# Two-layer graph network on one core: the sums over keys move from TensorE to DRAM gathers and VectorE

## The chip, the cores and the metric

The kernel runs on one core of a Trainium2 chip (trn2). The metric is the device time of one execution in microseconds (us), as the median of the runs. The engines are named as the profile has them: PE is TensorE (PEld its weight loads), DVE VectorE, ACT ScalarE, POOL GpSimd, SP SyncE, which here only issues DMAs (SPq is its queue).

## The reference

64 batch elements of 256 tokens with 512 features go through two layers. The first is multi-head attention under a mask, the second a graph attention with a rank-one score; both end in a residual and a layer norm. Everything is fp32.

```python
q, k, v = x @ Wq + bq, x @ Wk + bk, x @ Wv + bv        # 8 heads of 64
scores = einsum('bqhd,bkhd->bhqk', q, k) / 8 + (1 - adj) * -1e9
out = einsum('bhqk,bkhd->bqhd', softmax(scores), v) @ Wo + bo
x = layernorm(x + out)
h = x @ W
e = leaky_relu(s1[:, :, None] + s2[:, None, :], 0.2) * adj   # s1 = h @ a1, s2 = h @ a2
x = layernorm(x + elu(softmax(e) @ h + beta * h))
```

## The kernel before, in words

**Work and tiling.** Batch elements go in 32 pairs (m); an element is b = 2m + s. For a pair, `project` (L414) makes q, k and v, each 512 x 512 features on 512 tokens, with seven products of quarters in place of eight (sums and differences of quarters on both sides, as in Winograd's form of Strassen's scheme). The same helper is used per element for o (Wo), for spread (attention of the second layer times x) and for u (times W). The sums on the right side are made on GpSimd by `token_sums` (L393); the sums of weights once, at the start.

**Left sides.** Those of q and k are streamed: `streamed` (L358) makes four sums of quarters on DVE, stores them in DRAM, and from the second pair on each product fetches its left side (256 KB) into one of six slots named piece, in program names `wq_sums` and `wk_sums` (L381 from the weight itself, L386 from the stored sums). Wv, Wo and W stay in SBUF, with three sums each from `weight_sums` (L344, on POOL).

**First attention, by keys.** `scores` (L734) puts keys on partitions and queries in columns, so that exp of it, pT (8 heads of 128 x 2 x 256), can multiply v without a transpose. DVE adds the mask (L750), ACT takes the exponential (L752), POOL adds the two halves of keys into both (L754). The sum over the 128 keys on partitions is a product with ones: `denominators` (L758) runs eight matmuls into ps_den (L766), 32 columns wide, four at a time. Then DVE takes the reciprocal (L778), ACT adds up both for a check of range (L774, kept in range_sb), and the reciprocals go through DRAM to all partitions: rows<-inv (L786), inv_all<-rows (L790, two DMAs). ps_pv (L720) is pT times v; DVE multiplies it by inv_all (L816) into oT, POOL makes oS from it, and o follows. The last element takes another way without DRAM: ps_inv (L802).

**Second layer.** DVE makes the two scores of a token (L917), which go through DRAM to rows (L941, L943); e is formed on DVE, POOL and ACT (L946 to L966), transposed in blocks through DRAM (square L983, att_b L986, DVE L990), and used by spread. The last element has transposes on TensorE in place of both trips (L933, L976).

**What sets the order.** No scheduler of the compiler works here: all operations go into `Plan` (L54) with an engine, a cost in ns and what they read and write; `place` lists them. TensorE's order is fixed by turns: each operation has the round m + LATER[what] and its place in ROUND (L23); only its last 60 are free. The other engines take what can start, by due time counted back from TensorE's. A DMA is planned as landing 4.2 us after its issue. Every engine then executes its own list strictly in order, SP too: an issue that waits holds those behind it. Slots (L242) bound how far the lists run ahead; PSUM has 8 banks (`ps`), of which ps_sc takes two for each pair of heads, `project` three or four.

One line of code shows the product with ones:

```python
nc.tensor.matmul(acc[32 * c:32 * c + 32, :], ones[:, 16 - 16 * i:48 - 16 * i],
                 both[c][:, i, :], start=i == 0, stop=i == 1)
```

Of the kernel before, what the change touches and what calls it, by code (L numbers as in the profile page):

```python
# [12 lines left out]
ALU = mybir.AluOpType  # L13
# [3 lines left out]
P = 128  # L17
# [5 lines left out]
ROUND = ("sums1", "mix1", "scores0", "spread1", "v", "u1", "attention0", "sums0", "mix0", "scores1", "o1", "x",  # L23
         "logits1", "q", "spread0", "o0", "attention1", "u0", "k", "logits0")
# [3 lines left out]
         "u0": 1, "u1": 2}  # L28
SAFE = 1e15
# [198 lines left out]
def gnn_two_layers(ctx: ExitStack, tc: tile.TileContext, x, adj, Wq, bq, Wk, bk, Wv, bv, Wo, bo, W, a, beta, out):  # L228
# [13 lines left out]
    slots = {"xin": 2, "x": 4, "two": 6, "xP": 1, "piece": 6, "full": 4, "half": 18, "xS": 2, "st": 76, "ps": 8, "rows": 4, "svT": 4, "line": 4, "square": 4}  # L242
# [69 lines left out]
    wv_sb = weight(Wv, "wv_sb")  # L312
# [13 lines left out]
    range_sb = once([2, B], "range_sb")  # L326
    maskT_sb = once([NT, N], "maskT_sb")
# [30 lines left out]
    def streamed(w, w_dram, name):  # L358
# [4 lines left out]
        for n, to, p, m, op, reads in ((3, s3, w11, w21, ALU.subtract, [w]), (1, s1, w21, w22, ALU.add, [w]),  # L363
                                       (2, s2, s1, w11, ALU.subtract, [w, S[1]]),
                                       (4, s4, w12, s2, ALU.subtract, [w, S[2]])):
            plan.op("DVE", 700, lambda to=to, p=p, m=m, op=op: nc.vector.tensor_tensor(to(), p(), m(), op), reads,
                    [S[n]])
# [46 lines left out]
    def project(left, right, by_feature, claims, copy, add, inner=2, width=P, raw=False):  # L414
# [35 lines left out]
        if raw:  # L450
            add((0, 0), pe(2, second, True))
            copy((1, 0), pe(4, fourth, True))
        copy((1, 1), pe(5, cross, True))
        if not raw:
            add((0, 0), pe(2, second, True))
        copy((0, 1), pe(6, chain, False))
        add((0, 1), pe(3, cross, False))
        if not raw:
            copy((1, 0), pe(4, fourth, True) if second[1] is None else pe(4, fourth, False, [second]))
# [69 lines left out]
    def second_layer_constants():  # L529
        plan.op("POOL", 500, lambda: nc.gpsimd.memset(diag_sb[A], 0.0), [], [diag_sb])  # L530
# [53 lines left out]

    def pair(m, at, general=False):

        def turn(what):

            plan.turn = ((m or 0) + LATER[what], ROUND.index(what))
# [47 lines left out]
        def qk(left, bias, dst):  # L637
            project(left, right, True, [dst], *gather(
                lambda q: (lambda: dst[:, 2 * q[0]:2 * q[0] + 2, q[1] * N:(q[1] + 1) * N], (dst, q)), bias, True),
                width=N, raw=m == 0)  # L640

        if m == 0:
            wq_sb, wk_sb = sb("two", [C, D], "wq_sb"), sb("two", [C, D], "wk_sb")
            load(wq_sb, Wq)
            load(wk_sb, Wk)
            lq, left["q"] = streamed(wq_sb, Wq, "wq_sums")
# [7 lines left out]
            left["v"] = weight_sums(wv_sb, "sv_sb", "POOL")  # L654
            plan.turn = (0, ROUND.index("x"))
            left["o"] = residual_bias()
        else:
# [5 lines left out]
        project(left["v"], right, False, [V], *gather(  # L663
            lambda q: (lambda: V[:, 2 * q[1]:2 * q[1] + 2, half(q[0])], (V, q)), wide=True), width=N)
# [3 lines left out]
    def batch(m, s, qT, kT, V, dram, general):  # L668

        b = None if m is None else 2 * m + s  # L670
        last = b == B - 1 and not general
        X = sb("x", [NT, D], f"x_{b}")

        def turn(what):
            plan.turn = ((m or 0) + LATER[f"{what}{s}"], ROUND.index(f"{what}{s}"))
# [51 lines left out]
        def attention_by_keys():  # L727
# [6 lines left out]
            def scores(c):  # L734
# [4 lines left out]
                def pe():  # L739
                    for k in range(NT):  # L740
# [6 lines left out]
                        claims=pT[2 * c:2 * c + 2] + [both[c]])  # L747
                for i in range(2):
# [5 lines left out]
                    plan.op("POOL", 725, lambda h=h, i=i: nc.gpsimd.tensor_tensor(  # L754
                        both[c][:, i, :], pT[h][:, 0, :], pT[h][:, 1, :], ALU.add),
                        [pT[h]], [(both[c], i)])

            def denominators():  # L758
                turn("sums")

                acc = ps([N], "ps_den")

                def pe():
                    for i in range(2):
                        for c in range(C):
                            nc.tensor.matmul(acc[32 * c:32 * c + 32, :], ones[:, 16 - 16 * i:48 - 16 * i],  # L766
# [355 lines left out]
```

## Time and profile before

| | |
|---|---|
| median of 3 runs | 2732.69 us (2732.62 to 2733.25) |
| profiled execution, its own time | 2734.59 us |
| its span, first to last instruction | 2732.8 us |
| TensorE's granted clock, mean | 0.995 |
| busy: PE, DVE, POOL, ACT | 2698.5, 1960.9, 1728.6, 1549.5 us |
| DMA | 581,596 packets, 301.44 MB, q1 busy 41.7% of 16 engines |
| matmuls of ps_den (L766) | 1,024 records, 68.5 us busy |
| reciprocal of ps_den (L778) | 64 of 1,757 ns |

Busy time of matmuls overlaps from one to the next, and a record's end is modelled, so distances on TensorE are taken from start to start. A group's line gives its count, busy us and mean ns, then the engine's idle time just before it and who ended that. A matmul of fp32 with more than one pass shows as two records.

### The profile page before, as it was taken

How to read it: one execution, taken by the hardware profiler on the slowest of the kernel's cores; microseconds unless marked ns; L12 is line 12 of the kernel's file. 1: busy time of each engine (PE TensorE's matmuls, PEld its weight loads, DVE VectorE, ACT ScalarE, POOL GpSimd, SP SyncE). 2: the span in 40 equal slices, each digit the busy share in tenths (PEclk: the TensorE clock that was granted, in tenths of full speed). 3: DMA queues.
4: the chain of work that ended last, by engine and by line, in shares of the span. 5: the costliest groups of instructions: out<-in, count | busy, mean ns of one | idle time of the engine just before them, and what ended most of it. 6: DMA issues, size and time to landing. Idle time of an engine off the chain costs nothing. (4 is left out here: it accounts for less than half of the span.)

```text
span 2732.8 us, 47289 instructions
## 1 busy us (share of the span) xinstructions
PE 2698.5 (99%) x15897; PEld 2268.1 (83%) x15897; DVE 1960.9 (72%) x3676; ACT 1549.5 (57%) x3712; POOL 1728.6 (63%) x2261
## 2 busy tenths in 40 slices
PE   9999999999999999999999999999999999999996
PEld 7888888888888888888888888888888888888874
DVE  6777777777777777777777776777777777767674
ACT  3456556556556565565565565655655655656554
POOL 4756666665676666666656766666666566665663
PEclk9999999999999999999999999999999999999998
DMA  8434434344443444343443434443444434343211
GB/s 234 104 101 128 119 97 114 97 121 124 100 120 96 109 128 118 94 113 99 124 124 98 120 90 115 128 113 99 111 101 120 128 96 118 89 120 113 80 55 54
DMA packets 581596, 301.44 MB, mean 110 GB/s; under 512 B 407020, under 2 KB 512356, under 8 KB 581348
## 3 DMA queue, kind: packets, MB, share of 16 engines
q1 hardware_dynamic: 581220, 298.34, 41.7%
q8 instruction: 130, 2.13, 0.3%
q14 instruction: 118, 0.97, 0.1%
q0 software_dynamic: 128, 0.01, 0.0%
HBM read 245.50 MB, written 52.75 MB: 109 GB/s over the span
## 5 line engine op out<-in xcount | busy, mean ns | idle before, releaser
L754 POOL TENSOR_TENSOR both<-pT 128x256 f32<-128x256 f32 x512 | 361.3, 734 | 398.6 <-ACT pT L752 398.6
L750 DVE TENSOR_TENSOR pT<-ps_sc,maskT_sb 128x512 f32<-128x512 f32 x512 | 324.2, 680 | 84.7 <-PE ps_sc L743 84.7
L752 ACT ACTIVATE pT<-pT 128x512 f32<-128x512 f32 x512 | 304.0, 626 | 49.3 <-DVE pT L750 47.4
L917 DVE SCALAR_TENSOR_TENSOR junk<-x,wa_sb 128x512 f32<-128x512 f32 x256 | 207.8, 837 | 110.3 <-ACT x L581 109.2
L743 PE MATMUL ps_sc<-qT,kT 64*128 64x256 f32 x2048 | 238.4, 382 | 0.0
L720 PE MATMUL ps_pv<-pT,v 128*64 128x256 f32 x2048 | 235.1, 382 | 0.0
L743 PEld LDWEIGHTS ps_sc<-qT,kT 64*128 64x128 f32 x2048 | 192.8, 187 | 44.4 <-issue 24.6
L469 ACT COPY u<-ps_chain 128x256 f32<-128x256 f32 x126 | 47.0, 373 | 319.2 <-PE ps_chain L433 318.7
L581 ACT ACTIVATE x<-x,nmr,rs 128x512 f32<-128x512 f32 x256 | 197.6, 808 | 50.2 <-POOL nmr L577 50.0
L720 PEld LDWEIGHTS ps_pv<-pT,v 128*64 128x64 f32 x2048 | 141.3, 137 | 91.0 <-DVE kT L478 12.8
L1026 POOL TENSOR_TENSOR X_sums<-x 128x256 f32<-128x256 f32 x126 | 150.9, 1207 | 99.5 <-ACT x L581 99.5
L564 ACT ACTIVATE junk<-x,mean 128x512 f32<-128x512 f32 x256 | 182.2, 714 | 6.4 <-DVE mean L570 6.4
L564 ACT ACTIVATE junk<-x 128x512 f32<-128x512 f32 x256 | 159.4, 625 | 36.5 <-DVE x L894 33.7
L704 POOL TENSOR_TENSOR x<-x,res_sb 128x512 f32<-128x512 f32 x128 | 176.3, 1380 | 0.0
L575 POOL TENSOR_SCALAR rs<-sq 128x2 f32<-128x2 f32 x130 | 34.9, 269 | 194.3 <-ACT junk L564 189.0
L404 POOL TENSOR_TENSOR oS<-oT 128x256 f32<-128x256 f32 x126 | 92.1, 731 | 84.2 <-DVE mean L570 52.5
L816 DVE TENSOR_TENSOR oT<-oT,inv_all 128x512 f32<-128x512 f32 x126 | 134.7, 1107 | 0.0
L955 POOL TENSOR_TENSOR e<-e,adj_sb 128x512 f32<-128x512 f32 (+1 forms) x65 | 81.6, 1255 | 80.7 <-DVE e L952 76.8
L433 PE MATMUL ps_chain<-sw_sb,yS 128*128 128x256 f32 x504 | 129.3, 379 | 0.0
L433 PE MATMUL ps_chain<-so_sb,oS 128*128 128x256 f32 x504 | 129.3, 379 | 0.0
L778 DVE RECIPROCAL inv<-ps_den 128x256 f32<-128x256 f32 x64 | 112.5, 1757 | 17.1 <-PE ps_den L766 8.7
L404 POOL TENSOR_TENSOR yS<-yT 128x256 f32<-128x256 f32 x126 | 92.6, 735 | 48.5 <-DVE yT L478 32.2
(240 smaller groups left out, 7164.5 us busy)
## 6 DMA issues: line engine op xcount, KB each, us to landing
x<-in_x_dram SPq DMA_DIRECT2D x64, 512.0 KB
out_dram<-x SPq DMA_DIRECT2D x128, 256.0 KB
inv_all<-rows SPq DMA_DIRECT2D x126, 256.0 KB
xin<-in_x_dram SPq DMA_DIRECT2D x248, 128.0 KB
wq_sums<-wq_sums SPq DMA_DIRECT2D x124, 256.0 KB
wk_sums<-wk_sums SPq DMA_DIRECT2D x124, 256.0 KB
wq_sums<-in_L_gnn_Wq_dram SPq DMA_DIRECT2D x93, 256.0 KB
wk_sums<-in_L_gnn_Wk_dram SPq DMA_DIRECT2D x93, 256.0 KB
```

What stands on the lines that cost most here:

```text
L404: plan.op("POOL", 180 + 545 * width // P, lambda: nc.gpsimd.tensor_tensor(dst(), p(), m(), ALU.subtract), reads, writes)
L433: nc.tensor.matmul(dst[:, f, :], lhs, rhs, start=start and f == 0 and c == 0, stop=c == inner - 1, skip_group_check=True)
L564: plan.op("ACT", 700, lambda: nc.scalar.activation(junk[A], X[:, t, :], func, bias=mean[:, i:i + 1] if bias else 0.0, accum_out=to[:, i:i ...
L581: plan.op("ACT", 810, lambda i=i, t=t: nc.scalar.activation(X[:, t, :], X[:, t, :], AF.Identity, bias=nm[:, i:i + 1], scale=rs[:, i:i + 1] ...
L704: plan.op("POOL", 1270, lambda t=t: nc.gpsimd.tensor_tensor(X[:, t, :], X[:, t, :], res_sb[A], ALU.add), [res_sb], tokens(t))
L720: nc.tensor.matmul(acc[r * HD:(r + 1) * HD, i, :], V[:, 2 * k + s, h * HD:(h + 1) * HD], pT[h][:, k, :], start=k == 0, stop=k == NT - 1)
L743: nc.tensor.matmul(acc[j][:, k, :], kT[r:r + HD, c, key_blk(k)], own(qT, r, c), start=True, stop=True)
L750: plan.op("DVE", 690, lambda h=h, i=i: nc.vector.tensor_add(pT[h][A], acc[i][A], maskT_sb[A]), [acc[i], maskT_sb], [pT[h]])
L752: plan.op("ACT", 620, lambda h=h: nc.scalar.activation(pT[h][A], pT[h][A], AF.Exp, scale=1.0 / HD ** 0.5), [pT[h]], [pT[h]])
L754: plan.op("POOL", 725, lambda h=h, i=i: nc.gpsimd.tensor_tensor(both[c][:, i, :], pT[h][:, 0, :], pT[h][:, 1, :], ALU.add), [pT[h]], [(bot ...
L917: plan.op("DVE", 780, lambda t=t, i=i, junk=junk: nc.vector.scalar_tensor_tensor(junk[A], X[:, t, :], 1.0, wa_sb[:, i, :], op0=ALU.mult, o ...
L1026: plan.op("POOL", ns, lambda: nc.gpsimd.tensor_tensor(dst(), p(), m(), op), reads, writes)
```

## The change

- `denominators` no longer uses TensorE. The four tiles both (256 KB each) are written to DRAM as keys (128 keys x 2048 columns, a column is a head and a query). Four DMAs read them back with columns spread over partitions: few holds 32 keys x 64 columns on each partition, 32 column groups for each of four groups of keys, in runs of 64 elements (256 B). DVE adds up the 32 keys (part), which go through DRAM once more (parts, four) so that DVE can add the four groups and take the reciprocal of 64 x 32 numbers (den). Then rows and inv_all as before.
- The last pair (`near`) keeps the product with ones, straight from pT (16 matmuls for each element, no both), and both its elements have their logits and attention turned by TensorE, where before only the last element had.
- Left sides of v are streamed as those of q and k. wv_sb is a slot of two at the start only; the pieces have seven slots, not six.
- The first pair's products come in another order (`first`, before `raw`), its sums of weights too (s3 last), and diag_sb is cleared after w_sb has come.
- ROUND is another order.

```diff
-ROUND = ("sums1", "mix1", "scores0", "spread1", "v", "u1", "attention0", "sums0", "mix0", "scores1", "o1", "x",
-         "logits1", "q", "spread0", "o0", "attention1", "u0", "k", "logits0")
+ROUND = ("sums1", "mix1", "scores0", "v", "spread1", "o1", "u1", "logits1", "k", "attention0", "sums0", "mix0",
+         "scores1", "x", "q", "attention1", "spread0", "o0", "logits0", "u0")
...
-    slots = {... "piece": 6, ...}
+    slots = {... "piece": 7, ...
+             "keys": 3, "parts": 3, "few": 1, "part": 2, "four": 2, "den": 2}
...
-        if raw:
+        if first:
             add((0, 0), pe(2, second, True))
-            copy((1, 0), pe(4, fourth, True))
         copy((1, 1), pe(5, cross, True))
-        if not raw:
+        if not first:
             add((0, 0), pe(2, second, True))
         copy((0, 1), pe(6, chain, False))
-        add((0, 1), pe(3, cross, False))
-        if not raw:
-            copy((1, 0), pe(4, fourth, True) if second[1] is None else pe(4, fourth, False, [second]))
+        if not first:
+            add((0, 1), pe(3, cross, False))
+        copy((1, 0), pe(4, fourth, True) if second[1] is None else pe(4, fourth, False, [second]))
+        if first:
+            add((0, 1), pe(3, cross, False))
...
-            left["v"] = weight_sums(wv_sb, "sv_sb", "POOL")
+            lv, left["v"] = streamed(wv_sb, Wv, "wv_sums")
...
+        near = m == B // 2 - 1 and not general
...
             def denominators():
+                keys, parts = Buf(dram_pool, "keys", [P, H * N], "keys"), Buf(dram_pool, "parts", [4, H * N], "parts")
+                for c in range(C):
+                    plan.op("SP", 500, lambda c=c: nc.sync.dma_start(
+                        keys[:, 2 * c * N:2 * (c + 1) * N], both[c][A].rearrange("p i n -> p (i n)")), [both[c]],
+                        [(keys, c)])
+                few, part = sb("few", [32, 64], "few"), sb("part", [64], "part")
+                for g in range(4):
+                    plan.op("SP", 800, lambda g=g: nc.sync.dma_start(
+                        few[32 * g:32 * g + 32], keys[32 * g:32 * g + 32, :].rearrange("k (c n) -> c k n", n=64)),
+                        [keys], [(few, g)])
+                plan.op("DVE", 2200, lambda: nc.vector.tensor_reduce(
+                    part[A], few[A].rearrange("p k n -> p n k"), AX.X, ALU.add), [few], [part])
+                plan.op("SP", 500, lambda: nc.sync.dma_start(
+                    parts[A].rearrange("g (c n) -> (g c) n", n=64), part[A]), [part], [parts])
+                four, den = sb("four", [4, 32], "four"), sb("den", [2, 32], "den")
+                plan.op("SP", 500, lambda: nc.sync.dma_start(
+                    four[0:HD], parts[A].rearrange("g (c n) -> c g n", n=32)), [parts], [four])
+                plan.op("DVE", 210, lambda: nc.vector.tensor_reduce(
+                    den[0:HD, 0, :], four[0:HD].rearrange("p g n -> p n g"), AX.X, ALU.add), [four], [(den, 0)])
+                plan.op("DVE", 280, lambda: nc.vector.reciprocal(den[0:HD, 1, :], den[0:HD, 0, :]), [(den, 0)],
+                        [(den, 1)])
...
+                plan.op("SP", 500, lambda: nc.sync.dma_start(
+                    rows[A].rearrange("h (c n) -> (h c) n", n=32), den[0:HD, 1, :]), [(den, 1)], [rows])
+                to_all()
...
+            def denominators_near():
                 turn("sums")
...
-                plan.op("PE", 1000, pe, both, [acc], mode="sums", claims=[inv])
+                plan.op("PE", 1860, pe, pT, [acc], mode="sums", claims=[inv])
...
-            spread_inv = denominators()
+            spread_inv = denominators_near() if near else denominators()
...
-        if last:
+        if near:
             row = ps([N], "tr_s")
```

## The prediction

> **What bounds the kernel now.** I read the page's busy times and slices first, then the waits of TensorE, then the timeline of TensorE over a stretch in the middle, and last the groups for the lines that the diff touches. The page says TensorE is busy in every slice at its full clock, and no other engine is near that:
>
> ```profile
> span 2732.8 us, 47289 instructions
> PE 2698.5 (99%) x15897; PEld 2268.1 (83%) x15897; DVE 1960.9 (72%) x3676; ACT 1549.5 (57%) x3712; POOL 1728.6 (63%) x2261
> PE   9999999999999999999999999999999999999996
> PEclk9999999999999999999999999999999999999998
> ```
>
> "Busy" alone proves little, since matmuls overlap. The list of what TensorE waited for is better evidence: its longest entries sum to some 19 us in 2733, and every one lies in the first 90 us or the last 90 (us in total, times, longest):
>
> ```profile
> PE tr_x L608 <- DMA xin<-in_x_dram: 4.1, 2, 3.7
> PE ps_inv L802 <- DVE select L783: 2.8, 1, 2.8
> PE ps_chain L433 <- DVE attT L990: 2.5, 1, 2.5
> PE ps_fourth L433 <- POOL xS L404: 2.0, 1, 2.0
> ```
>
> So in the 31 rounds between, TensorE's own instructions set the time: a round (two batch elements) is 83.65 us, from one ps_sc at 2515.90 to that of the next round at 2599.55. An instruction taken from TensorE there shortens the run by what it occupies, as long as nothing else becomes late. What the sums over keys occupy is read from start to start (the second column, a duration, overlaps the next row):
>
> ```profile
> 1002.20 1.89 PE L433 MATMUL ps_fourth<-xS,wk_sums 128*128 128x256 f32 x8
> 1003.93 1.89 PE L433 MATMUL ps_chain<-xS,wk_sums 128*128 128x256 f32 x8
> 1005.75 1.07 PE L766 MATMUL ps_den<-both,ones 128*32 128x256 f32 x16
> 1006.75 3.67 PE L720 MATMUL ps_pv<-pT,v 128*64 128x256 f32 x32
> 1010.36 3.72 PE L743 MATMUL ps_sc<-qT,kT 64*128 64x256 f32 x32
> ```
>
> ps_den holds TensorE from 1005.75 to 1006.75: 1.00 us. The other place in the round, 1035.48 to 1036.48, gives 1.00 too.
>
> **What the Trainium skill says.** "TensorEngine Tiling (Array Packing)", Key Properties: a change of tiling mode drains TensorE. The trace agrees: a plain product takes 1.73 us from start to start, the one ahead of ps_den 1.82. That 0.09 stays, since ps_pv has a mode of its own: at 2653.70 a product of half the size goes straight into ps_pv and takes 0.96 against 0.86. "TensorE: Matmul & The Clock Gate" (Architectural detail) says that VectorE executes in strict order; so a VectorE instruction that waits for a DMA holds up all behind it. No row of before shows that for a long wait. "DMA: Bandwidth & Descriptors", Anatomy of one DMA, gives about 2 us fixed cost for a DMA; here rows<-inv is issued at 1038.43 and inv_all<-rows, which waits for it, at 1040.31: 1.88 us. Its Specifications name 512 B as the least transfer for full rate; the prices worked out below agree in kind: 128 B in 13.7 ns are 9 bytes a ns, 1.4 KB in 72.7 ns are 20.
>
> **The change part by part.** *Removed from TensorE.* 62 of the 64 batch elements lose ps_den: 62 x 1.00 = **-62.0 us**, all on the path. The last two keep it, on pT with twice the matmuls: at most 2 x 1.00 = **+2.0**. The round's other products are the same in number and shape, and the built order still changes mode into ps_pv, into ps_sc and back.
>
> *VectorE.* A reciprocal of 1.757 us goes. In come a reduction of 64 x 32 elements, one of 32 x 4 and a small reciprocal. The reduction at L957 has 675 ns for 512 elements and 410 for 256, so 1.035 ns an element: 675 + 1536 x 1.035 = 2.27 us, then 0.28 and 0.17. Net +0.96 per element, 59 us in all; VectorE goes from 1961 to 2020 us, 76% of the shorter span. ScalarE's two sums get shorter. Nothing here is on the path by its sum.
>
> *DMA engines.* Price of a packet: the DMA view of the stretch 1057 to 1070 has 8,424 packets under 512 B and 1,002 larger at 90.4% busy (188 us of engine time); the whole run has 407,020 and 174,200 at 41.7% (18,234 us). Two equations give 13.7 ns for a small (128 B) and 72.7 ns for a large one. A 256-byte packet lies between; by its bytes 19 ns (the large ones hold 1.4 KB on average: 301.44 MB less the small ones, over 174,200). Per round the change adds 1,024 large ones for keys, 8,192 of 256 B for few, 1,280 large for the seven left sides of v, and some 900 small: 74 + 159 + 93 + 15 = 341 us over 16 engines, 21.3 us. A stretch of 85 us in the middle shows a share of 0.44, thus 36.8 us a round; after it 58 of 81.65 us, **71%**. With few's packets at 72.7 ns it would be 85.4 us, more than a round.
>
> *SyncE's queue.* 27 more issues in a round: 7 pieces at 0.35 us, 8 keys at 0.38 (as square), 8 few at 0.63 (as att_b), 4 small at 0.5: 12.5 us. Its waits sum to about 1,790 us of 2733, 55 us a round, so they fit. It works in order: behind the wait of parts for the reduction stand square, att_b and the pieces of k or q.
>
> *The chain of a denominator.* From the start of the heads' products: both (8 x 0.73 on GpSimd, behind the exponentials) about 9 us; six hops of DMA at 1.9 to 2.1 us, 12; few's own transfer, 4,096 x 19 / 16 = 5; VectorE 2.7; then the product with inv_all 2 x 1.1 and oS 4 x 0.73. About 34 us. The new order gives 62 us between scores0 and o0, and 53 between scores1 and o1 (sums of start-to-start times: v, q, k 12.1 each, o and u 6.05, spread 3.1, ps_sc 3.65, ps_pv 3.61). Queues can double every hop and it still fits. The pieces: a slot frees when the product seven before has run; the nearest case, k to q, leaves 10.4 + 7.3 = 17.7 us where a load takes about 3. Before, six slots for seven products left only 5 x 1.73 = 8.6 us, and no wait is shown. So I take **+4 us** in all for new stalls, from 0 (the stretch has no wait now that could go) to 116 (the slower rival).
>
> *Start.* The fourth product moves behind those that need fewer of GpSimd's sums of x: up to 2.04 (the wait) and 3.66 - 1.89 (the products after it ran slow), -3.8 in all. Against it, the DMA engines are 83.2% busy in the first 80 us, and the sums of wv, keys and few add over 20 us of work to them. I take **-1**, from -4 to +10.
>
> *End.* The last ps_den comes ahead of ps_pv, not behind it: 2654.66 to 2658.26, so 3.6 us earlier, and the 2.8 us wait of ps_inv is covered; but ps_den is longer and batch 62 has its logits by TensorE. I take **-3**, from -8 to +4.
>
> Sum: -62 + 2 + 4 - 1 - 3 = **-60**. The profiled execution took 2734.59 us, 2732.8 of it the span; less 60, 2674.6. The median of the runs shown is 2732.69, 1.9 lower, so I say **2672 us** (-2.2%). About 0.2% can be told from no change here.
>
> **Rivals.** *Late gathers stall part of it.* At 71% mean share the DMA queue has bursts: ahead of few stand three or four keys, six pieces and three xin. If each of the two reductions in a round waits 0.6 us longer than the PSUM buffers cover, 62 x 0.6 = 37 comes back: **2707**. For: in-order VectorE, and xin issues that already took 3.03 us at worst against a median of 0.66. Against: 20 us and more of slack above.
>
> *Slower: VectorE blocked behind few.* The reduction waits for four DMAs in the middle of the adds that empty PSUM for o0 (behind scores1) and u1 (behind scores0). It decides against the change from 1.0 us of TensorE's time per reduction, since 62 x 1.0 is the whole gain. If a 256-byte packet costs as much as a large one, few takes 4,096 x 72.7 / 16 = 18.6 us, the gathers of scores1 land after their place in VectorE's order, and the DMA engines' 85.4 us become the round: 31 x (85.4 - 81.65) = 116 on top, **2788**. For: the share, and that VectorE has no way round the wait. Against: xin and att_b at 128 B cost 13.7 ns.
>
> *No effect.* If ps_den's place were filled by a wait that is now hidden under it, such as ps_pv for the last pT, the time stays near **2733**. Against: ps_den needs the same exponentials and a GpSimd sum on top, so ps_pv was ready before it.
>
> **How the numbers follow.** Forecast (2658 to 2690) 0.65; part stalled (2690 to 2727) 0.20; no effect 0.03; slower 0.12. Faster 0.85, same 0.03, slower 0.12. The low end takes the best start and end with no stall: 2732.7 - 62 + 2 - 4 - 8 = 2661, less the 0.1% by which 83.65 and 1.00 us are rounded. The high end, 2725, covers nearly all of the second case; slower and no effect stay out.
>
> **What would show it.** Right: L766's successor has only 32 records in the last 100 us; rounds of about 81.65 us from ps_sc to ps_sc; no new entry among TensorE's waits between 100 and 2550 us; DMA share near 0.70; the reduction of few near 2.27 us. Wrong: VectorE idle ahead of part<-few with the DMA few<-keys as releaser, TensorE waiting for VectorE's adds, rounds above 82.5 us, or a 256-byte packet dearer than 30 ns.

## The result and the profile after

The changed kernel takes **2833.06 us** (median of 4 runs, 2828.74 to 2845.86) against 2732.97 for the kernel before in the same job: ratio 1.0372, 95% interval 1.0337 to 1.0406. It is 3.7% slower; the forecast was 2672. One of the four executions of a run below, e16, took 5073 us for a reason that wasn't traced, and its ratio leaves that one out. The profiled execution took 2831.58 us, its span is 2829.4. Of the page of the changed kernel:

```profile
span 2829.4 us, 47451 instructions
PE 2688.5 (95%) x14943; PEld 2253.6 (80%) x14943; DVE 2110.4 (75%) x3805; ACT 1505.0 (53%) x3713; POOL 1695.0 (60%) x2243
PE   8899999999999999999999999999999999999998
DMA packets 946184, 492.88 MB, mean 174 GB/s; under 512 B 700544, under 2 KB 828808, under 8 KB 945928
q1 hardware_dynamic: 945800, 489.76, 67.8%
L794 DVE TENSOR_REDUCE part<-few 128x64 f32<-128x2048 f32 x62 | 228.1, 3679 | 106.4 <-DMA few<-keys 103.5
```

TensorE has 954 matmul records less and still 95% where it had 99%; from the third slice on each digit looks as before, since a loss of 4% doesn't move a tenth. The waits say where it went. TensorE's of the changed kernel (us in total, times, longest):

```profile
PE ps_pair L435 <- DVE u L481: 88.5, 28, 4.6
PE ps_chain L435 <- ACT u L472: 13.7, 29, 0.8
```

and VectorE's own:

```profile
DVE part L794 <- DMA few<-keys: 103.5, 31, 5.3
```

31 waits for 62 reductions: 29 of them stand behind scores1, in nearly every round; the reduction after scores0 waits only twice in the run and finds few in place otherwise. One such stall, in VectorE's timeline of the changed kernel (start, duration, then what it waited for):

```profile
1043.55 0.41 DVE L941 TENSOR_TENSOR x<-x,ps_chain 128x256 f32<-128x256 f32 x1
1047.41 3.64 DVE L794 TENSOR_REDUCE part<-few 128x64 f32<-128x2048 f32 x1 [3.46 <-DMA few<-keys]
1050.97 0.48 DVE L1013 SCALAR_TENSOR_TENSOR e<-e,rc,diag_sb 128x256 f32<-128x256 f32 x1
1051.36 0.42 DVE L941 TENSOR_TENSOR x<-x,ps_pair 128x256 f32<-128x256 f32 x1
```

VectorE stands still for 3.46 us and then reduces for 3.64, in the middle of the additions that empty the PSUM tiles of o (x<-x,ps_...). TensorE fills the tiles it has left and stops:

```profile
1048.99 1.03 PE L435 MATMUL ps_cross<-sw_sb,yT 128*128 128x256 f32 x4
1053.26 2.04 PE L435 MATMUL ps_pair<-w_sb,yS 128*128 128x256 f32 x4 [3.23 <-DVE u L481]
1055.09 1.91 PE L435 MATMUL ps_chain<-sw_sb,yS 128*128 128x256 f32 x4
1056.94 4.81 PE L732 MATMUL ps_pv<-pT,v 128*64 128x256 f32 x32
1061.68 3.72 PE L755 MATMUL ps_sc<-qT,kT 64*128 64x256 f32 x32
```

From start to start, ps_cross to ps_pair is 4.27 us where such a product takes 0.87: 3.4 lost. Then the next three take 1.83, 1.85 and 4.74 where 0.87, 0.96 and 3.61 are usual: 3.0 more. The Trainium skill, "TensorE: Matmul & The Clock Gate" (What's actually happening), says that TensorE's clock falls to half after an idle window of about 3.4 us and rises again after a busy one, and that the windows run freely, so that the moment varies. The trace's record of the granted clock has 0.50 from 1052.46 to 1059.29 here: 3.2 us of idleness are followed by 6.0 us at half speed, and the gap is paid nearly twice.

Not every gap is. Between 190 and 2690 us TensorE has 27 gaps of over 1.5 us ahead of this product. The clock record has a stretch at half speed at 17 of them, 14 of 3.4 us and 3 of 6.8, 68 us in all, which cost at most half of that, 34 us; at the gap of 3.68 us that ends at 1405.97 there is none. Most of the loss is the waits themselves, 88.5 us for u.

**The ledger** (from ps_sc to ps_sc, both spans): two first rounds and what lies ahead of them +14.8 us (188.75 against 173.91); 29 rounds +92.1 (86.8 against 83.64 each); the end -10.3 (122.9 against 133.25). Sum +96.6, the difference of the spans.

### The profile page after: what moved, and what is told of

Its sections match the earlier page's. It is cut to its first block, busy times and chain, and to the rows that moved or that the text cites. A ratio compares the mean times of both kernels' runs of the same rounds, so it can differ in the third digit from the quotient of the medians.

```text
span 2829.4 us, 47451 instructions
## 1 busy us (share of the span) xinstructions
PE 2688.5 (95%) x14943; PEld 2253.6 (80%) x14943; DVE 2110.4 (75%) x3805; ACT 1505.0 (53%) x3713; POOL 1695.0 (60%) x2243
## 3 DMA queue, kind: packets, MB, share of 16 engines
q1 hardware_dynamic: 945800, 489.76, 67.8%
## 4 chain that ended last, share of the span: by engine, by line
PE 72%; DVE 9%; DMA 8%; SPq 4%; issue 3%; POOL 3%; ACT 1%; POOLq 0%; DVEq 0%; ACTq 0%
PE ps_chain L435 24%; PE ps_cross L435 15%; PE ps_pv L732 8%; PE ps_sc L755 8%; DMA few<-keys 7%; PE ps_second L435 6%; PE ps_fourth L435 5%; PE ps_pair L435 5%; DVE part L794 4%; SPq L791 4%; DVE z L993 2%; DVE x L941 2%; POOL e L1002 1%; DMA keys<-both 1%; POOL X_sums L1073 1%
## 5 line engine op out<-in xcount | busy, mean ns | idle before, releaser
L767 POOL TENSOR_TENSOR both<-pT 128x256 f32<-128x256 f32 x496 | 391.2, 820 | 205.4 <-ACT pT L764 205.4
L794 DVE TENSOR_REDUCE part<-few 128x64 f32<-128x2048 f32 x62 | 228.1, 3679 | 106.4 <-DMA few<-keys 103.5
L578 POOL TENSOR_SCALAR rs<-sq 128x2 f32<-128x2 f32 (+1 forms) x130 | 34.4, 265 | 416.4 <-ACT junk L567 408.3
L1073 POOL TENSOR_TENSOR X_sums<-x 128x256 f32<-128x256 f32 x126 | 108.4, 861 | 275.6 <-ACT x L584 275.6
L567 ACT ACTIVATE junk<-x,mean 128x512 f32<-128x512 f32 x256 | 183.1, 717 | 26.3 <-POOL e L1002 23.7
L716 POOL TENSOR_TENSOR x<-x,res_sb 128x512 f32<-128x512 f32 x128 | 160.6, 1276 | 0.0
L435 PE MATMUL ps_pair<-w_sb,yS 128*128 128x256 f32 x252 | 75.7, 428 | 89.2 <-DVE u L481 88.5
L435 PE MATMUL ps_chain<-sw_sb,yS 128*128 128x256 f32 x504 | 145.9, 416 | 13.7 <-ACT u L472 13.7
L406 POOL TENSOR_TENSOR oS<-oT 128x256 f32<-128x256 f32 x126 | 102.9, 816 | 82.0 <-DVE oT L863 77.1
L435 PEld LDWEIGHTS ps_pair<-w_sb,yS 128*128 128x128 f32 x252 | 49.3, 206 | 106.5 <-issue 100.5
L435 PEld LDWEIGHTS ps_chain<-sw_sb,yS 128*128 128x128 f32 x504 | 99.5, 205 | 42.3 <-ACT u L472 28.4
```

The lines of the kernel that those rows point to most:

```text
L435: nc.tensor.matmul(dst[:, f, :], lhs, rhs, start=start and f == 0 and c == 0, stop=c == inner - 1, skip_group_check=True)
L567: plan.op("ACT", 700, lambda: nc.scalar.activation(junk[A], X[:, t, :], func, bias=mean[:, i:i + 1] if bias else 0.0, accum_out=to[:, i:i ...
L716: plan.op("POOL", 1270, lambda t=t: nc.gpsimd.tensor_tensor(X[:, t, :], X[:, t, :], res_sb[A], ALU.add), [res_sb], tokens(t))
L794: plan.op("DVE", 2200, lambda: nc.vector.tensor_reduce(part[A], few[A].rearrange("p k n -> p n k"), AX.X, ALU.add), [few], [part])
L1073: plan.op("POOL", ns, lambda: nc.gpsimd.tensor_tensor(dst(), p(), m(), op), reads, writes)
```

## The experiments

Theories: **A**, late gathers and the reduction together block VectorE for longer than PSUM covers; **B**, the transfers alone set the time; **C**, the chain of the denominators is late further on, at oT. The expectation of e1 uses A and B for the gathered reduction against streaming and order, and that of e2 calls the transfers C. "Round" is the mean of 20 rounds in the middle, from the first ps_sc of the seventh pair to that of the twenty-seventh; it is 83.64 in the kernel before and 87.0 in the changed one. All ratios are to the kernel before in the same job.

| run | median us | ratio, 95% interval | round us |
|---|---|---|---|
| e1 sums by PE | 2757.64 | 1.0080, 1.0063 to 1.0097 | 84.53 |
| e2 reduce later | 3009.97 | 1.0996, 1.0978 to 1.1015 | 92.8 |
| e3 eighth of the gather | 2704.63 | 0.9882, 0.9865 to 0.9898 | 82.82 |
| e4 short reduction | 2723.95 | 0.9951, 0.9935 to 0.9968 | 83.5 |
| e5 tree of additions | 2831.43 | 1.0347, 1.0330 to 1.0364 | 86.4 |
| e6 reduction on GpSimd | 2928.09 | 1.0727, 1.0688 to 1.0767 | 89.8 |
| e7 long runs | 2957.81 | 1.0810, 1.0792 to 1.0828 | 90.7 |
| e9 old round | 2955.68 | 1.0794, 1.0769 to 1.0818 | 91.0 |
| e10 bf16 gather | 2707.20 | 0.9898, 0.9882 to 0.9915 | 82.8 |
| e11 true landing | 2876.74 | 1.0515, 1.0498 to 1.0533 | 88.8 |
| e13 new round alone | 2774.41 | 1.0145, 1.0128 to 1.0162 | 84.53 |
| e14 split reduction | 2834.62 | 1.0378, 1.0354 to 1.0403 | 86.9 |
| e15 bf16, old round | 2898.40 | 1.0593, 1.0575 to 1.0611 | 88.7 |
| e16 no v pieces | 2873.35 | 1.0508, 1.0487 to 1.0529 | 88.8 |
| e17 xin after | 2737.65 | 1.0009, 1.0001 to 1.0018 | 82.8 |
| e18 xin after, tree | 2810.50 | 1.0272, 1.0252 to 1.0291 | 85.9 |

### What each part costs by itself

**e1**: `denominators` as before the change (eight matmuls on both), all else changed.

> The changed kernel with the sums over keys back on TensorE (both times ones, as before); v stays streamed, the new order of rounds and of first products stays. Theory A (the gathered reduction in VectorE's strict order is the whole loss): rounds of 83.65 us as before, 2730 to 2750 us. Theory B (the loss comes from streaming v or from the new order of rounds): well above 2780 us, with the same gaps of TensorE.

**e13**: the kernel before with the new ROUND as its only edit.

> The kernel before with the changed kernel's order of rounds alone: sums over keys on TensorE, v's left sides resident, first products as before. The changed kernel with its sums given back to TensorE took 0.9 us more per round than before, and its first rounds 17 us more. If the order of rounds makes the 0.9 us: 2757 us (2745 to 2765) with the beginning as before. If the streaming of v makes it: within 5 us of before, 2734.

e1 lies 8 us above the range of its first theory, and its rounds aren't those of before. The rounds of e1 and e13 are equal, 84.53 us: the new order costs 0.89 us a round, and streaming v costs nothing there. Where, the timeline of TensorE in e13 shows:

```profile
1006.60 1.03 PE L433 MATMUL ps_cross<-so_sb,oT 128*128 128x256 f32 x4
1007.90 1.10 PE L433 MATMUL ps_pair<-wo_sb,oS 128*128 128x256 f32 x4 [0.27 <-DVE x L894]
1008.84 1.03 PE L433 MATMUL ps_chain<-so_sb,oS 128*128 128x256 f32 x4
```

In the new order spread, o and u come one after another, 21 short products whose results must be taken out of PSUM, and TensorE waits 0.27 us for VectorE in this round. Summed from start to start over eight middle rounds, o's products take 0.4 us more per round than in the kernel before and u's another 0.4. e13 came out above its own range, 17 us slower than e1 although its first rounds are 5 us shorter; that lies in its last stretch (146.8 us, in e1 125.0), which I didn't trace.

### Wait or length

**e3**: few brings 4 of 32 keys, the rest are ones; sums of part of the keys, so the denominators differ from the reference's.

```diff
-                        few[32 * g:32 * g + 32], keys[32 * g:32 * g + 32, :].rearrange("k (c n) -> c k n", n=64)),
+                        few[32 * g:32 * g + 32, 0:4],
+                        keys[32 * g:32 * g + 4, :].rearrange("k (c n) -> c k n", n=64)),
```

> The gather brings 4 of 32 keys on each partition; the other 28 are a constant 1 in SBUF, so the sums are not those of the reference. The reduction is as long as in the changed kernel and stands in the same place of VectorE's list. If the late landing is what counts, its wait of 3.3 us vanishes and the time falls to 2680 to 2720 us; if the length of the reduction (3.7 us) is enough by itself to run PSUM full, 2780 us or more.

**e4**: the gather whole, the reduction over 4 of 32 keys (`few[:, 0:4]`); denominators again of part of the keys.

> The gather is whole, but the reduction adds up only 4 of 32 keys on each partition, so the sums are not those of the reference; it takes about 0.6 us and stands in the same place. If the wait for few alone (3.3 us) runs PSUM full: 2770 us or more. If it takes wait and length together: 2680 to 2730 us, with the wait still in VectorE's list.

Both came out as theory A has it, and both are clean: VectorE, GpSimd and ScalarE execute the same instructions in the same order as in the changed kernel. e3 has the full reduction at its old place and no wait for few, and TensorE's wait for VectorE's u is gone. e4 has the whole wait (109.3 us for few in 30 times) and a reduction of 0.60 us, and TensorE waits 13.1 us for u in all; 0.7 us a round are left against e3. So PSUM covers a reduction of 3.7 us, and nearly a wait of 3.6, and not both. Two runs make the reduction itself cheaper: **e5** (tree) and **e14** (two halves).

```diff
-                plan.op("DVE", 2200, lambda: nc.vector.tensor_reduce(
-                    part[A], few[A].rearrange("p k n -> p n k"), AX.X, ALU.add), [few], [part])
+                def tree():
+                    n = 16
+                    while n:
+                        nc.vector.tensor_add(part[A].unsqueeze(1) if n == 1 else few[:, 0:n, :], few[:, 0:n, :],
+                                             few[:, n:2 * n, :])
+                        n //= 2
+
+                plan.op("DVE", 2700, tree, [few], [few, part])
```

```diff
+                for i in range(2):
+                    plan.op("DVE", 1850, lambda i=i: nc.vector.tensor_reduce(
+                        part[:, 32 * i:32 * i + 32], few[:, :, 32 * i:32 * i + 32].rearrange("p k n -> p n k"), AX.X,
+                        ALU.add), [few], [(part, i)])
```

> The reduction over 32 keys is made of five contiguous VectorE additions (1024, 512, 256, 128 and 64 elements) in place of one TENSOR_REDUCE that reads at a stride of 256 bytes; nothing else is changed. Theory A (the gap of TensorE comes when late gathers and a long reduction add up in VectorE's order, and exceed what PSUM covers): 1984 elements at the 1.035 ns of contiguous reads and five starts of some 0.06 us are 2.4 us in place of 3.68, so the gap of 3.2 us a round falls to about 1.9 and the slow clock after it with it; some 2 to 2.5 us a round, 2770 us (2750 to 2800). Theory B (the gap is the late gather alone, the length of the reduction doesn't count): within 5 us of the changed kernel, 2828 to 2838. Theory C (denominators that come late further on set the time): also near 2830.

> The reduction is cut into two of 32 columns each (half as long), and the planner may put other VectorE work between them; gathers unchanged. Theory A: what stands behind the wait is 1.85 us instead of 3.68, the gap of 3.2 us falls by at most that much: 2780 us (2755 to 2810). If shortening brings as little as the tree of additions did (0.7 us shorter, same time), because the planner moves the late DMA to another place: 2815 to 2840.

Both missed A's number. The tree takes 3.03 us, not 2.4 (1275 ns for 1024 elements down to 233 for 64: some 0.2 us a start), so it saves 0.65, but the wait for few grew to 118.8 us; the middle rounds fell by 0.6, and slower first rounds took that back. The halves of e14 stand back to back, or with one instruction of a quarter us between them, behind each wait, so VectorE is blocked as long as before; and in its plan both gathers of a round come late (148.9 us in 60 times).

### Another place for the reduction

**e2** holds both reductions back by a turn of TensorE that does nothing; **e11** only corrects the planner's figures; **e6** makes the reduction on GpSimd (the tree of e5 with `nc.gpsimd.tensor_tensor`).

```diff
+                plan.turn = (m, ROUND.index("logits1")) if not s else (m + 1, ROUND.index("sums1"))
+                plan.op("PE", 0, lambda: None, [], [(part, "turn")], claims=[part])
```

```diff
-                        [keys], [(few, g)])
-                plan.op("DVE", 2200, lambda: nc.vector.tensor_reduce(
+                        [keys], [(few, g)], lag=3500)
+                plan.op("DVE", 3700, lambda: nc.vector.tensor_reduce(
```

> The changed kernel, but both reductions of few stand later in VectorE's list: behind the u products of their stretch, where before the one of scores1 stood in the middle of the adds of o0. Nothing else is edited. Theory A: the wait for few and the gap of TensorE after it vanish, rounds of 82 to 83 us, 2680 to 2710 us. Theory C (the DMA engines cannot carry the gathers and set the pace wherever the reduction stands): 2790 us or more.

> Only the planner's figures change: the gathers land 3.5 us later in its reckoning (7.7 us after the issue in place of 4.2) and the reduction is 3.7 us in place of 2.2, so that it puts the reduction and the additions where the chip can meet them. Theory A (the plan sends VectorE to the reduction too early): the wait for few falls from 3.4 us per round to under 1, and with it TensorE's wait for u: 2750 us (2710 to 2790). Theory C (the chain has no room: what is put later here is late at oT): the wait for few goes, but waits for inv_all or oT take its place, 2800 to 2900.

> The reduction is made on GpSimd (five additions), so that no wait for the gathers and no long reduction stands in VectorE's order; gathers, DMAs and the order of the work stay. Theory A: TensorE no longer waits for VectorE's u; rounds fall from 86.9 to about 82.8 us, as with the short gathers: 2705 us (2690 to 2740), if the reduction on GpSimd (some 5.6 us from its additions of 256 elements in 0.7 us) makes the denominators at most 3 us later. Theory C (the chain of a denominator has no slack left, each us that it comes later is a wait for oT): the reduction ends 2 us later, TensorE waits about as much per round for oS or yT, 2770 to 2830. Theory B (transfers): waits on the gather move to GpSimd and cost nothing, 2705 as well.

All three are slower than the changed kernel: e11 within C's range, e6 above it, e2 far above what A expected (its other theory said 2790 or more). TensorE's wait for VectorE's u shrinks or goes, and a dearer one comes. e11's waits of TensorE and of VectorE, and one place in the timeline:

```profile
PE ps_chain L437 <- ACT yT L474: 132.3, 30, 6.6
```

```profile
DVE oT L865 <- DMA inv_all<-rows: 51.1, 28, 4.5
```

```profile
1614.85 1.74 DVE L865 TENSOR_TENSOR oT<-oT,inv_all 128x512 f32<-128x512 f32 x2 [2.02 <-DMA inv_all<-rows]
1616.66 0.37 ACT L474 COPY yT<-ps_chain 128x256 f32<-128x256 f32 x1 [6.60 <-DVE oT L865]
1617.18 1.19 PE L437 MATMUL ps_chain<-att_sums,X_sums 128*128 128x128 f32 x4 [4.68 <-ACT yT L474]
```

The reciprocals reach all partitions after VectorE is ready to multiply. ScalarE's copy of spread's first result into yT starts 0.07 us after the last of these products, and TensorE, which needs that result out of PSUM, after the copy; 127.8 of the 132.3 us have this form. yT isn't made from oT, but in the code both yT and inv_all are tiles named full, of which there are four, and oT's products are the only readers of inv_all. So what the copy waits for is, as far as code and times tell, the slot that inv_all gives back; no run had a fifth. e2 shows the same, 170.6 us for yT in 31 times. e6 waits at the same place (72.7 us in 19 times), and for GpSimd's own sums (yS, 18.5 us) behind a reduction of 5.4 us.

So C holds in part as soon as the reduction is moved: earlier it waits for few; later oT comes late, and what waits for oT is spread. Two remedies are open: more slots full, which wasn't tried, and earlier gathers.

### The transfers

**e7**: runs of 512 bytes, eight DMAs of 16 partitions.

```diff
-                few, part = sb("few", [32, 64], "few"), sb("part", [64], "part")
-                for g in range(4):
-                    plan.op("SP", 800, lambda g=g: nc.sync.dma_start(
-                        few[32 * g:32 * g + 32], keys[32 * g:32 * g + 32, :].rearrange("k (c n) -> c k n", n=64)),
+                few, part = sb("few", [16, 128], "few"), sb("part", [128], "part")
+                for g in range(8):
+                    plan.op("SP", 500, lambda g=g: nc.sync.dma_start(
+                        few[16 * g:16 * g + 16], keys[16 * g:16 * g + 16, :].rearrange("k (c n) -> c k n", n=128)),
```

> The gather brings 128 columns of 16 keys to a partition (2048 packets of 512 bytes for a reduction in place of 4096 of 256), in eight DMAs of 16 partitions in place of four of 32; the reduction has as many elements at a stride of 512 bytes. Theory A: the gathers occupy the DMA engines 2 us less per reduction but take some 2 us more to issue, so few lands 0 to 2 us earlier and the gap shrinks by as much; 2800 us (2765 to 2835). Theory B: as A, with the wait for few alone setting the time, 2790 to 2835. If the stride rather than the count of elements makes the reduction slow, it takes longer than 3.68 us, and the time is 2830 or more.

Worse than any theory: the wait ahead of the reduction grew to 196.5 us (106.4 in the changed kernel), though there were half as many gather packets. Their records in the trace show one reason: a gather's packet of 512 bytes took 70 ns in the mean, one of 256 bytes in the changed kernel 24.9, so a gather is 2048 x 70 / 16 = 9 us in place of 4096 x 24.9 / 16 = 6.4. The length alone isn't what makes them dear, since the other 512-byte packets of e7, from part to parts, took 27 ns; the gather's DMAs also fill 16 partitions each, not 32, and that wasn't tried by itself. With eight more DMAs a round in SyncE's list the plan differs too. (The profile names xin and v's pieces as releasers for most of this wait; the reduction itself reads few alone.)

**e10**: both, few and, likewise, keys in bfloat16; nothing left out, the sums of the reduction in float32, rounding of bfloat16 in the denominators.

```diff
-            both = [sb("half", [2, N], "both") for c in range(C)]
+            both = [sb("half", [2, N], "both", BF16) for c in range(C)]
...
-                few, part = sb("few", [32, 64], "few"), sb("part", [64], "part")
+                few, part = sb("few", [32, 64], "few", BF16), sb("part", [64], "part")
```

> What is gathered is held in bfloat16 (both, keys and few), the reduction's result in float32: half the bytes to write and to gather, as many packets of half the size, every instruction where it was; the denominators carry the rounding of bfloat16. Theory A (TensorE's gap is the time by which the gathers land too late, added to the reduction): 0.5 MB of writes and about 3 us of packet time less in the burst, so few lands some 4 us earlier, in time, as with an eighth of the keys: rounds of 83 us, 2715 us (2700 to 2745). Theory B (the number of DMAs that SP issues and the chain of six hops set it): 2815 to 2840.

A's number: 2707.20. As many DMAs, every instruction in the order of the changed kernel, the reduction as long (3715 ns; "VectorE: DVE Perf Modes", The perf-mode tier table, has no faster mode for it, and none is seen), half the bytes. VectorE's wait for few is gone (1.2 us in the whole run), and the longest of TensorE's waits is that of e3:

```profile
PE ps_chain L437 <- ACT u L474: 15.1, 29, 0.6
```

With e3, e4 and e10 the cause of the stall is shown: the gathers land late and the reduction is long, and either alone costs little.

Whose transfers, then? SyncE's queue in the changed kernel, from the first keys to the gathers (scores1 started at 1020.50):

```profile
1024.01 0.43 SPq L714 DMA_DIRECT2D x<-in_x_dram  x1
1024.55 3.08 SPq L785 DMA_DIRECT2D keys<-both  x3
...
1030.75 0.32 SPq L785 DMA_DIRECT2D keys<-both  x1
1031.36 0.88 SPq L388 DMA_DIRECT2D wv_sums<-wv_sums  x1
1032.34 1.36 SPq L629 DMA_DIRECT2D xin<-in_x_dram  x2
1033.79 2.62 SPq L388 DMA_DIRECT2D wv_sums<-wv_sums  x1
1036.45 0.59 SPq L629 DMA_DIRECT2D xin<-in_x_dram  x1
1037.14 0.61 SPq L383 DMA_DIRECT2D wv_sums<-in_L_gnn_Wv_dram  x1
1037.85 4.58 SPq L791 DMA_DIRECT2D few<-keys  x4
...
1043.88 5.50 SPq L629 DMA_DIRECT2D xin<-in_x_dram  x5
```

Between 1024 and 1052 the packets' times sum to 98% of what 16 engines have; between 1037 and 1048 even to 119%, so records overlap, and such a share says only that much is in flight. **e16** leaves v's pieces out from the second pair on (one constant tile in their place, so v isn't the reference's). Its edit also takes the slots of piece from seven to six, which its expectation doesn't say.

> From the second pair on, v's left sides are one constant tile instead of seven pieces brought per round (values of v are then not the reference's, all instructions else are there); the gather is whole, in float32. That takes 1.75 MB per round out of the transfers, seven DMAs of which are issued between the scores and the gathers. If v's pieces in the same burst make the gathers late: the wait for few goes, rounds of 82.8 to 84 us, 2720 us (2700 to 2745). If the gathers' own bytes and those of keys and xin make it: rounds stay above 86, 2810 to 2835.

Slower than the changed kernel and outside both ranges. The wait for few stays, 125.4 us. SyncE's queue in e16 tells why it is no proof against A:

```profile
1047.76 0.44 SPq L788 DMA_DIRECT2D keys<-both  x1
...
1049.84 0.62 SPq L629 DMA_DIRECT2D xin<-in_x_dram  x1
1050.57 1.27 SPq L388 DMA_DIRECT2D wk_sums<-wk_sums  x1
1051.90 3.26 SPq L629 DMA_DIRECT2D xin<-in_x_dram  x2
1055.26 4.15 SPq L794 DMA_DIRECT2D few<-keys  x4
```

Pieces of k and more of xin moved into the room, so what v's pieces cost stays open. Then **e17** leaves all in and holds xin back until the reduction after scores1 of the pair two before has been made, which falls in the same round:

```diff
+            before = [summed[m - 2]] if m is not None and m > 1 else []
             for f in range(4):
                 plan.op("SP", 700, lambda f=f: nc.sync.dma_start(
-                    xb[f * 32:(f + 1) * 32].rearrange("p c (b i) -> p c b i", i=32), rows[f]), [], [(xb, f)])
+                    xb[f * 32:(f + 1) * 32].rearrange("p c (b i) -> p c b i", i=32), rows[f]), before, [(xb, f)])
...
+                if s == 1 and m is not None:
+                    summed[m] = part
```

> The eight xin loads of a round wait for the second reduction of the round (a dependence on its result), so that they no longer stand ahead of the gathers; everything in float32, nothing left out. Three of the eight stood ahead of the gathers: 3072 packets of 13 ns on 16 queues are 2.5 us, and 2 us of issue. If traffic ahead of the gathers makes them late: they land 2.5 to 4 us earlier, the wait for few falls from 3.4 to under 1 us per round, rounds of 83 to 84.5 us, 2740 us (2715 to 2775). If the gathers' own bytes make it: wait within 1 us of before, 2815 to 2840. The small hops behind the reduction now queue behind xin; if that makes oT late, TensorE waits there instead, 2780 to 2850.

2737.65 us, within A's range: 95 us less than the changed kernel, by one dependence that holds back eight loads, all in float32 and complete. The plan built with it orders other instructions differently as well, so the run isn't as clean as e3 and e10; but the reduction still stands behind the fourth addition of o. SyncE's queue (scores1 at 996.75) and VectorE there:

```profile
1007.26 0.32 SPq L787 DMA_DIRECT2D keys<-both  x1
1007.77 1.88 SPq L389 DMA_DIRECT2D wv_sums<-wv_sums  x2
1011.06 0.38 SPq L384 DMA_DIRECT2D wv_sums<-in_L_gnn_Wv_dram  x1
1012.52 2.86 SPq L793 DMA_DIRECT2D few<-keys  x4
```

```profile
1019.40 0.42 DVE L945 TENSOR_TENSOR x<-x,ps_chain 128x256 f32<-128x256 f32 x1 [0.44 <-PE ps_chain L436]
1020.40 3.67 DVE L796 TENSOR_REDUCE part<-few 128x64 f32<-128x2048 f32 x1 [0.58 <-DMA few<-keys]
1023.99 0.41 DVE L945 TENSOR_TENSOR x<-x,ps_pair 128x256 f32<-128x256 f32 x1
```

From the start of scores1 few lands after 23.7 us in place of 26.9. Of the 3.2, 1.8 come ahead of the first gather (5.3 from the last keys to it, was 7.1) and 1.7 in the four issues (2.86, was 4.58), less 0.3 by which keys came later; from their end to the landing it is 5.0 in both. Three pieces of v stand there in both kernels; the three xin are what left. VectorE's wait for few is 29 us in all (103.5 before), and the middle rounds, 82.8 us, are those of e3. What keeps e17 33 us above e3 lies ahead of them: 13 us in the first two rounds and what lies ahead of them, 14 in the eight rounds after.

**e18** is e17 with the tree.

> As the run before, with the reduction as five contiguous additions (2.97 us in place of 3.68, as measured). If traffic ahead of the gathers makes them late: 5 to 10 us less than the run before, 2732 us (2710 to 2770). Otherwise within 10 us of it.

It missed: its rounds alternate between 82.7 and 88 to 90 us, with waits for yT (34.4) and VectorE's x (31.9) in every second. The tree took 3.0 us behind scores1, but 4.2 to 4.4 behind scores0, longer than the one reduction. And another cost in the plan gave another order everywhere; I didn't trace which step made it.

### The order of rounds

**e9** is the changed kernel with the old ROUND, **e15** is e10 with it.

> The changed kernel with the order of rounds of the kernel before (sums still gathered through DRAM, v streamed, first products in the new order). The old order leaves a whole round between the scores of the second batch and its output product, and the new one 13 of 20 steps. Theory A: what counts is which PSUM-emptying additions stand behind the reduction in VectorE's order; that changes by chance, 2790 us (2740 to 2840). Theory C (the window of the second denominator is what makes it late): 2720 to 2760. If the new order is what the gathered sums need, the old one is slower than the changed kernel, above 2840.

> The bfloat16 gather with the order of rounds of the kernel before. The new order alone took 84.53 us per round against 83.64, and the gathered sums 1.73 less than the sums on TensorE. If the gathers now land in time in the old order too: rounds of 81.9 us, 2685 us (2670 to 2700). If the old order lacks room between the scores and their output product for the first batch, TensorE waits there as in the run with the old order and float32 (90.9 us per round): 2720 to 2900.

Both were slower, as their last theories had it. TensorE's timeline in e15, with what ScalarE and VectorE did just before it went on:

```profile
1007.85 0.61 PE L437 MATMUL ps_pair<-attT,x 128*128 128x128 f32 x4
1011.56 1.19 PE L437 MATMUL ps_chain<-att_sums,X_sums 128*128 128x128 f32 x4 [3.11 <-POOL both L769]
```

```profile
1009.15 1.82 DVE L865 TENSOR_TENSOR oT<-oT,inv_all 128x512 f32<-128x512 f32 x2
1011.05 0.37 ACT L474 COPY yT<-ps_chain 128x256 f32<-128x256 f32 x1 [1.14 <-DVE oT L865]
```

Spread follows scores0 at once in the old order and waits 3.1 us in every round. The profile puts that down to GpSimd's both, but the sums that spread needs of GpSimd had been made 7.6 us earlier, while ScalarE's copy into yT ended 0.14 us before TensorE went on, and began 0.08 us after VectorE's oT. It is the wait of e11 again: spread needs yT's slot, and oT comes too late for it, here behind the eight additions of the mask. e9 has the same 3.1 us. So in these plans the gathered sums go with the new order, whose 0.89 us is part of their price; whether the old order with another slot would do was not tested.

## Why the prediction was wrong

- **-62 us on TensorE: right in kind.** From e1 to e3 a round loses 84.53 - 82.82 = 1.71 us, to e10 about the same; predicted 2.00. Over 31 rounds -53. (In e3 and e10 TensorE still waits half a us a round for u.)
- **"The new order" was given no cost of its own.** e13: +0.89 a round, 26 us in 29. The step said that products are the same in number and shape, and put the order at nothing; it didn't ask whether three short projections in a row still find free PSUM.
- **The chain of a denominator is the step that failed: "about 34 us" of "53", "Queues can double every hop and it still fits", hence +4 us of stalls.** In the round shown: last keys issued 10.3 us after scores1 starts (predicted 9 for both), first gather at 17.4, landed at 26.9 (predicted about 18), reduced at 30.6, den begun at 40.9, rows issued at 41.7, inv_all at 47.4, oT begun at 54.5, o at 60.2. Hops were counted at a price read in a stretch without a burst (and the section of the Trainium skill that the prediction names for about 2 us is on DMAs issued from GpSimd, while SyncE issues these); waiting for a turn in VectorE's list (10 us from reduction to den, with VectorE at other work or waiting for TensorE's; four had come by then, since den waits 0.3 us for it in the whole run) wasn't counted at all. And slack at o1 is the wrong slack: the reduction had a *place* in VectorE's order, fixed by a plan that took 4.2 us per DMA, and was late against that place. Stalls, by the ledger: 92.1 - 29 x 0.89 + 29 x 1.71 = 116 us, 4.0 a round, against +4 in all. TensorE's wait for u is 88.5 of that, and the half clock can explain the rest (at most 34).
- **Which rival.** The slower one named the mechanism (VectorE in order, waiting in the middle of the adds that empty PSUM) and the threshold of about 1 us per reduction; 4.0 a round is twice that. Its reason was off: the DMA engines were no round of 85 us (67.8% busy), and the packets no 72.7 ns. The records of the gathers' packets have 24.9 ns in the mean, and 26.9 in the burst shown, where the prediction took 19: there few takes 4,096 x 26.9 / 16 = 6.9 us, not 4.9. The partial rival had the list of what stands ahead of few, xin included, and gave it 0.6 us.
- **The reduction: 3.68 us, not 2.27.** Its price came from a reduction along contiguous elements. Busy VectorE came out at 2110 us, not 2020: 62 x 1.41 = 87. The prediction said that nothing there is on the path by its sum; by its place it was.
- **SyncE.** The issues fit by number, but four gathers take 4.58 us to issue in this burst, against 2.5 counted from 0.63 each.
- **Start -1, measured +14.8.** e1 shows +6.5 without the gathers (180.46 against 173.91), so the rest is gathers and stalls in the first rounds. **End -3, measured -10.3**, in e10 -10.9, and -8.3 in e1, so the gathers aren't what makes it. e13, with the new order and the old end, loses 13.5 there; which edit of the last pair wins it back wasn't separated.

The question that would have turned the forecast was at hand: how long does all take that SyncE's built order puts between keys and the gathers, and where does the reduction stand in VectorE's built order by then?

A version that beats both is e10 (2707.20 us, ratio 0.9898, so 1.0% under before), with denominators gathered in bfloat16. In float32, e17 is level with before. Open: why e17's first rounds take up to 6 us more than its later ones, why e18's order is worse, what v's pieces cost the gathers, and what a fifth slot full would change.

## What to carry to other kernels

A transfer that an in-order engine waits for must be timed against its place in that engine's list, in the burst in which it runs; slack at the final consumer and mean shares of a queue say nothing of it. When such a step is late where it is, and moving it makes another wait, look at what else is issued ahead of its transfer: holding back loads with a round to spare gained 95 us. And before a wait is put down to the engine that the profile names, see whether that engine had long made what is needed: in e15 it was, as far as code and times tell, a tile's slot.

## What the runs showed of the hardware

- A float32 reduction over the outer axis of a tile takes 1.72 ns an element ((3679 - 597) ns for 1792 elements more, changed kernel against e4), whether elements lie 256 or 512 bytes apart (3679 and 3653 ns) or 128 in bfloat16 (3715), against 1.02 along contiguous ones (675 - 414 ns for 256, kernel before).
- A gap of 2.4 to 4.6 us in TensorE's work was followed by half the granted clock, for 3.4 us or for 6.8, at 17 of 27 gaps of the changed kernel; at others, of up to 3.7 us, the clock stayed.
- SyncE needs 2.9 us for four gathers in one burst (e17) and 4.6 in a fuller one (changed kernel): issue time is no constant.
- DMA packets of the gathers took 13 ns with 128 bytes (e10), 24.9 with 256 (changed kernel) and 70 with 512 (e7, where a DMA also fills 16 partitions in place of 32). The 512-byte packets from part to parts took 27 ns in the same run.
